# Layer 0's clamps of two sequences on GpSimd, and half of a folding sum in pieces between earlier matmuls, in a bidirectional minGRU and ternary feed-forward kernel

## The chip, the cores and the metric

The kernel runs on one core of a Trainium2 chip. The core has five engines with instruction lists of their own: TensorE (PE in the profile; its weight loads are PEld), VectorE (DVE), ScalarE (ACT), GpSimd (POOL) and SyncE (SP, which here only issues transfers). Engines wait for each other by semaphores. The metric is the device time of one execution in microseconds (us), lower being better; times given are medians of several runs.

## The reference

The input `x` is 8 sequences of 512 positions with 512 features, all in float32. Two stages are added to it.

```python
def _mingru(x, Wz, bz, Wh, bh):
    z = sigmoid(x @ Wz.T + bz)
    h_tilde = tanh(x @ Wh.T + bh)
    a = clip(1.0 - z, 1e-8, 1.0 - 1e-8)
    return linear_scan(a, z * h_tilde)        # h[s] = a[s] * h[s-1] + b[s]

def _stack(x):                                # four layers
    h = x
    for i in range(4):
        h_new = _mingru(h, W[i], b[i], W[i], b[i])
        if i > 0:
            h_new = h_new + h
        h = layernorm(h_new, gamma, beta)
    return h

n = layernorm(x)
h = concat(_stack(n), flip(_stack(flip(n))))  # forwards and backwards
x = x + h @ fusion_W.T + fusion_b
f = gelu(layernorm(x) @ ternary(W_fc).T)
x = x + (layernorm(f) * ln_w + ln_b) @ ternary(W_proj).T
```

Both gates of a layer use the same weights and bias, so one product `u` serves both, and forwards and backwards use the same weights too: in layer 0 they differ only in the direction of the scan. `ternary` rounds weights to -1, 0 and 1 by the mean of their absolute values.

## The kernel before

**Tiles.** A state is a tile of 128 partitions with 4 chunks of 512: the features lie along partitions (chunk `c` holds features 128c to 128c + 127), the 512 positions along the free dimension. A chunk of a layer is four matmuls of 128x128 by 128x512 in float32, added up in one PSUM tile `u` (L459 in layers 1 to 3, L504 in layer 0). The pool of these tiles, `ps_u`, has four buffers (L229). ScalarE makes the three factors from `u` (L476 to L478): `a`, the sigmoid of the negated sum, then `t`, the tanh, and `z`, the sigmoid. VectorE clamps `a` to the reference's limits (L482), multiplies `z` by `t` (L483) and scans (L487).

**Layer 0** (`first_layer`, L491) does not normalise `x` itself. Its weights are centred beforehand (L716), and VectorE multiplies `u` by the row of reciprocal deviations, `scale`, on its way out of PSUM (L515); the factors are then made from that SBUF tile. One set of factors serves a forward scan into `zf` and a backward scan into `z`. The three steps of a chunk stand in different slots: the matmuls in one, `scaled` later (by two slots for sequence 1), and `scans` one after that.

**The layer norm between layers** turns tiles of features into tiles of tokens: TensorE transposes four 128x128 blocks into a PSUM tile `pt` (L314), VectorE takes mean and variance (`stats`, L169 to L180), GpSimd raises the variance to the power -0.5 (L176, one number a partition), ScalarE writes the normalised `tok` (L186, L187), TensorE transposes back into `pf` (L323) and ScalarE applies gamma and beta (L329).

**Order.** The order of every engine's list is written out by hand by `slot` (L437): the matmuls of a chunk, then what is due by kind (`factors`, `late`, and so on), then shares of the transposes of other states, then scans, then the ends of the shares. Each engine works through its list in order. `first_layer(0)` and `first_layer(1, 2)` are run first (L728), then layers 1 to 3 of sequences 0 and 1, forwards and backwards in turn: the states are called (0, 0), (0, 1), (1, 0) and (1, 1).

**The folding.** gamma and beta of the last layer norm are folded into the fusion's weights. For each half `d` of these weights, `fold_sums` (L667) multiplies them by a tile `both` that repeats beta and gamma 64 times each (L730), four matmuls of 128x512 into one `u` buffer, and ScalarE copies the result to a `tok` tile. In the kernel before, the two halves are done behind layer 1 of states (0, 0) and (0, 1) (L763).

**Loads.** SP issues nearly all loads. A queue of eight semaphores is reused in turn, so each issue also waits for the landing of the load eight places before it. gamma and beta (2 KB each) stand behind sequence 1's rows and its transposed input (L147 to L151).

Of the kernel before, what the change touches and what calls it, by code (L numbers as in the profile page):

```python
# [16 lines left out]
P = 128  # L17
# [7 lines left out]
def kernel(  # L25
# [114 lines left out]
    for first, second in (  # L140
# [3 lines left out]
        for q, (load, at) in ((nc.scalar, first), (nc.sync, second)):  # L144
            load(q, at)
    nc.sync.dma_start(out=gb, in_=gru_b)
    for t in range(NT):  # L147
        load_x("n", 1, t)
    load_xT(1)
    nc.sync.dma_start(out=gam, in_=gamma)  # L150
    nc.sync.dma_start(out=bet, in_=beta)  # L151
    fw = fusp.tile([P, 2 * NC_, H], F32, name="fw")
    nc.sync.dma_start(out=fb, in_=fus_b.broadcast_to([P, H]))
    nc.sync.dma_start(out=fw, in_=fus_wT.rearrange("(c p) h -> p c h", p=P))
# [72 lines left out]
    with rec:  # L227
# [209 lines left out]
        def slot(work=None, cap=1, long=False):  # L437

            end = work() if work is not None else None
            due("factors")  # L440
            due("late")
            if long:
                due("scans")
            last = shares(cap) + x_shares()
            due("scans")
            if end is not None:
                end()
            due("resid")
            for f in last:
                if f is not None:  # L450
                    f()
            now[0] += 1
# [25 lines left out]
            nc.scalar.activation(z, u, AF.Sigmoid, bias=gb[:, l, o : o + 1])  # L478
            return a, t

        def product(a, z, t):
            nc.vector.tensor_scalar(a, a, CLAMP_HI, CLAMP_LO, ALU.min, ALU.max)  # L482
            nc.vector.tensor_tensor(z, z, t, ALU.mult)  # L483

        def scan(dst, a, z, backward):
# [5 lines left out]
        def first_layer(b, lag=0):  # L491
# [4 lines left out]
            def chunk(o):  # L496
                def work():
                    while zlive[0] + 2 > ZT:
                        slot(None, 2)
                    zlive[0] += 2  # L500
                    name = f"{b}_0_{o}"
                    u = ps_u.tile([P, S], F32, tag="u", name=f"u_{name}")
                    for c in range(NC_):
                        nc.tensor.matmul(  # L504
                            u, lhsT=gw[0][:, c, ts(o, P)], rhs=xT[b][:, c, :],
                            start=(c == 0), stop=(c == NC_ - 1),
                        )
                        if (b, o, c) in midway:
                            midway.pop((b, o, c))()

                    wait = 1 if (b, o) == (0, 0) else 0

                    def scaled():
                        z = zp.tile([P, S], F32, tag="z", name=f"z_{name}")
                        nc.vector.tensor_tensor(z, u, scale[b], ALU.mult)  # L515
                        a, t = factors(z, z, 0, o, name)

                        def scans():
                            product(a, z, t)
                            f = zp.tile([P, S], F32, tag="z", name=f"zf_{name}")  # L520
                            scan(f, a, z, False)
                            zf.append(f)
                            if o == NC_ - 1:
                                state[b, 0] = xT.pop(b)
                                norm((b, 0), zf, f"{b}0_0", 2 if b == 1 else 1, 2 if b < 2 else 1)

                            def backward():
                                scan(z, a, z, True)
                                zb.append(z)
                                if o == NC_ - 1:  # L530
                                    norm((b, 1), zb, f"{b}1_0", 2 if b == 1 else 1, 2 if b < 2 else 1)
                            if b == 0:
                                stages.append((now[0] + 1, "resid", backward))
                            else:
                                backward()
                        stages.append((now[0] + 1 - wait, "scans", scans))
                    stages.append((now[0] + lag + wait, "factors", scaled))
                return work
# [125 lines left out]

        folded = {}

        def fold_sums(d):  # L667

            ps = ps_u.tile([P, H], F32, tag="u", name=f"pfold_{d}")
            for c in range(NC_):  # L670
                nc.tensor.matmul(
                    ps, lhsT=both[:, c, :, :].rearrange("p i r -> p (i r)"), rhs=fw[:, d * NC_ + c, :],
                    start=(c == 0), stop=(c == NC_ - 1),
                )
            folded[d] = tokp.tile([P, H], F32, tag="tok", name=f"fold_{d}")
            held[0] += 1
            nc.scalar.copy(folded[d], ps)

        def fold(d):

# [44 lines left out]
        take(xturns)  # L725
        midway[0, 1, 0] = lambda: take(xbacks)()
        f0, f1 = first_layer(0), first_layer(1, 2)
        for i, work in enumerate(f0 + f1):  # L728
            slot(work, 4 if i == NC_ + 1 else 2, i > NC_ + 1)
        for i, v in enumerate((bet, gam)):  # L730
            nc.vector.tensor_copy(both[:, :, i, :], v.unsqueeze(2).broadcast_to([P, NC_, 64]))
        for b in range(0, B, 2):
            last_pair = b + 2 == B
            if b == 0:
# [9 lines left out]
            for l in range(1, L):  # L744
# [5 lines left out]
                for s in ((b, 0), (b, 1), (b + 1, 0), (b + 1, 1)):  # L750
# [9 lines left out]
                    if last_pair and s == (b, 0) and l == L - 1:  # L760
                        norm_y(0)
                    layer(s, l)
                    if b == 0 and l == 1 and s[0] == 0:  # L763
                        fold_sums(s[1])
                    if b == 0 and l == 2:
                        if s[0] == 0:
                            fold(s[1])
# [263 lines left out]
```

## Time and profile before

| | before |
|---|---|
| median of 3 runs | 1717.03 us (1716.73 to 1717.18) |
| profiled execution, whole | 1717.09 us |
| its span, first to last instruction | 1715.1 us |
| TensorE busy | 1703.4 us (99%) |
| VectorE busy | 1452.0 us (85%) |
| ScalarE busy | 1073.7 us (63%) |
| GpSimd busy | 214.0 us (12%) |

Four kinds of view are used. The page gives sums for the whole span. The chain of work that ended last gives, from the last instruction backwards, what each step waited for; its lines are start, length, engine and line. The timeline gives an engine's instructions in order of time: start, length, engine, line, operation, output and inputs, shapes, how many of them follow each other, and in brackets the idle time before and what ended it. A matmul in float32 is two records of half its work. Its end is modelled, so an idle time of TensorE is a little longer than the bracket says. The windows give busy times of all engines by stretch:

```profile
20.00:36.00 16.00, 16.00 (x53) 8.12 (x52) 14.46 (x29) 9.59 (x21) 2.48 (x5) 1.00 0.87 317
36.00:52.00 16.00, 13.43 (x60) 7.73 (x59) 15.16 (x35) 14.38 (x27) 4.17 (x6) 1.00 0.00 1
52.00:71.00 19.00, 18.82 (x56) 8.88 (x55) 18.59 (x26) 14.87 (x28) 0.00 (x0) 1.00 0.09 28
71.00:91.80 20.80, 19.36 (x75) 10.26 (x74) 19.39 (x48) 17.99 (x36) 4.82 (x8) 1.00 0.04 13
91.80:110.00 18.20, 18.20 (x81) 10.83 (x80) 13.70 (x35) 15.63 (x30) 3.62 (x6) 1.00 0.10 31
```

The columns are the stretch and its length, busy time and number of instructions of PE, PEld, DVE, ACT and POOL, the granted TensorE clock as a share, the mean share of the DMA engines and the rate in GB/s. In the first 92 us VectorE is busy over 90% of the time, and TensorE has pauses from 36 us on; behind that TensorE has none.

### The profile page before, as it was taken

Reading aid. Unit: us, or ns where it says so; the run is one execution under the profiler, and the core shown is the slowest. Engines: PE = TensorE matmul, PEld = TensorE weight load, DVE = VectorE, ACT = ScalarE, POOL = GpSimd, SP = SyncE. Lnnn points to the kernel's source line nnn. Section 1 sums busy time; section 2 is a strip of 40 time slices with the busy share of each in tenths; the row PEclk is TensorE's granted clock in tenths of the full one; section 3 lists DMA queues with packets and bytes.
Section 4 is the critical chain, followed back from the end, with each engine's and each line's share of the span. In section 5 each row is a group of like instructions: output and inputs, shape, how many; then the busy total and the mean of one; then the engine's idle time right before and its main releaser. Section 6 shows DMA issues by size and latency. Waiting matters only on the chain.

```text
span 1715.1 us, 19769 instructions
## 1 busy us (share of the span) xinstructions
PE 1703.4 (99%) x6440; PEld 1042.3 (61%) x6440; DVE 1452.0 (85%) x2863; ACT 1073.7 (63%) x1856; POOL 214.0 (12%) x334
## 2 busy tenths in 40 slices
PE   9999999999999999999999999999999999999999
PEld 4455554555555445555545555554688888888887
DVE  7989989889998998999899899996568768768877
ACT  5898873468886246888624688860366566566654
POOL 2111111111111111111111111110000000000000
PEclk9999999999999999999999999999999999999999
DMA  7002221160000115000011201202201101100100
GB/s 270 19 25 81 99 86 43 56 202 1 1 13 19 56 56 202 1 1 18 14 55 68 105 9 41 74 1 96 76 1 49 50 0 50 49 16 35 50 19 32
DMA packets 46599, 91.75 MB, mean 53 GB/s; under 512 B 5280, under 2 KB 5536, under 8 KB 45472
## 3 DMA queue, kind: packets, MB, share of 16 engines
q1 hardware_dynamic: 45488, 88.78, 15.1%
q10 hardware_dynamic: 1008, 1.70, 0.3%
q8 instruction: 51, 0.84, 0.2%
q14 instruction: 52, 0.43, 0.1%
HBM read 65.30 MB, written 25.17 MB: 53 GB/s over the span
## 4 chain that ended last, share of the span: by engine, by line
PE 87%; DVE 10%; ACT 1%; issue 1%; DMA 1%; POOL 0%; DVEq 0%; ACTq 0%
PE u L459 32%; PE po L870 14%; PE ph L843 14%; PE pu L586 12%; PE pt L314 6%; PE u L504 5%; PE pf L323 4%; DVE z L487 3%; DVE st L169 1%; DVE z L483 1%; PE py L212 1%; DVE zf L487 1%; DVE z L552 1%; DVE a L482 1%; DVE mv L171 0%
## 5 line engine op out<-in xcount | busy, mean ns | idle before, releaser
L459 PE MATMUL u<-h,gw 128*128 128x512 f32 x768 | 345.5, 592 | 0.0
L459 PE MATMUL u<-xT,gw 128*128 128x512 f32 x768 | 345.4, 593 | 0.0
L487 DVE TENSOR_TENSOR_SCAN z<-a,z 128x512 f32<-128x512 f32 x224 | 274.1, 1224 | 7.6
L459 PEld LDWEIGHTS u<-h,gw 128*128 128x128 f32 x768 | 138.7, 190 | 139.2 <-issue 138.9
L459 PEld LDWEIGHTS u<-xT,gw 128*128 128x128 f32 x768 | 138.7, 190 | 139.2 <-issue 138.2
L476 ACT ACTIVATE a<-u,ngb 128x512 f32<-128x512 f32 x192 | 131.6, 685 | 142.4 <-PE u L459 141.8
L169 DVE BATCH_NORM_STATS2 st<-pt 128x6 f32<-128x512 f32 x256 | 177.2, 692 | 40.8 <-PE pt L314 40.3
L176 POOL TENSOR_TENSOR rs<-ve,mhalf 128x1 f32<-128x1 f32 x192 | 122.7, 639 | 703.7 <-DVE nmu L180 665.4
L870 PE MATMUL po<-pwq,ghi 128*128 128x512 f32 x512 | 202.7, 396 | 0.0
L843 PE MATMUL ph<-yhi,fcq 128*128 128x512 f32 x512 | 199.7, 390 | 0.0
L870 PE MATMUL po<-pwq,glo 128*128 128x512 f32 x512 | 199.6, 390 | 0.0
L843 PE MATMUL ph<-ylo,fcq 128*128 128x512 f32 x512 | 199.4, 389 | 0.0
L847 ACT ACTIVATE g<-ph 128x512 f32<-128x512 f32 x128 | 76.4, 597 | 186.4 <-PE ph L843 186.4
L483 DVE TENSOR_TENSOR z<-z,t 128x512 f32<-128x512 f32 x224 | 153.4, 685 | 9.4 <-ACT z L478 9.4
L187 ACT ACTIVATE tok<-pt,nmr,rs 128x512 f32<-128x512 f32 x192 | 149.2, 777 | 6.4
L858 DVE TENSOR_TENSOR acc<-acc,g 128x512 f32<-128x512 f32 x112 | 77.3, 690 | 84.7 <-ACT g L847 83.8
L478 ACT ACTIVATE z<-u,gb 128x512 f32<-128x512 f32 x192 | 132.2, 689 | 0.0
L477 ACT ACTIVATE t<-u,gb 128x512 f32<-128x512 f32 x192 | 130.7, 681 | 0.0
L314 PEld LDWEIGHTS pt<-ident,z 128*128 128x128 f32 x640 | 78.6, 141 | 80.2 <-issue 47.5
L504 PE MATMUL u<-xT,gw 128*128 128x512 f32 x256 | 115.0, 593 | 1.0 <-DVE gw L716 0.8
L586 PE MATMUL pu<-fw,xT 128*128 128x512 f32 x256 | 115.2, 593 | 0.0
L586 PE MATMUL pu<-fw,h 128*128 128x512 f32 x256 | 115.1, 592 | 0.0
(150 smaller groups left out, 2559.8 us busy)
## 6 DMA issues: line engine op xcount, KB each, us to landing
xf<-in_x_dram SPq DMA_DIRECT2D x32, 256.0 KB, 5.8
x<-xf SPq DMA_DIRECT2D x32, 256.0 KB, 2.0
xy<-x SPq DMA_DIRECT2D x32, 256.0 KB, 4.1
xn<-in_x_dram SPq DMA_DIRECT2D x31, 256.0 KB, 4.5
out_dram<-xy SPq DMA_DIRECT2D x31, 256.0 KB, 2.0
xT<-in_xt_dram SPq DMA_DIRECT2D x7, 1024.0 KB, 7.5
fca<-in_fc_wT_dram SPq DMA_DIRECT2D x16, 256.0 KB, 3.0
pwa<-in_proj_wT_dram SPq DMA_DIRECT2D x16, 256.0 KB, 2.7
```

The lines of the kernel that those rows point to most:

```text
L169: nc.vector.bn_stats(st, src)
L187: nc.scalar.activation(dst, src, AF.Identity, bias=nmr, scale=rs)
L314: nc.tensor.transpose(pt[:, ts(c, P)], zs[c][:, ts(t, P)], ident)
L459: nc.tensor.matmul(u, lhsT=gw[l][:, c, ts(o, P)], rhs=h[:, c, :], start=(c == 0), stop=(c == NC_ - 1),)
L476: nc.scalar.activation(a, u, AF.Sigmoid, bias=ngb[:, l, o : o + 1], scale=-1.0)
L478: nc.scalar.activation(z, u, AF.Sigmoid, bias=gb[:, l, o : o + 1])
L483: nc.vector.tensor_tensor(z, z, t, ALU.mult)
L487: nc.vector.tensor_tensor_scan(dst[:, d], a[:, d], z[:, d], 0.0, ALU.mult, ALU.add)
L504: nc.tensor.matmul(u, lhsT=gw[0][:, c, ts(o, P)], rhs=xT[b][:, c, :], start=(c == 0), stop=(c == NC_ - 1),)
L586: nc.tensor.matmul(pu, lhsT=hs[d][:, c, ts(t, P)], rhs=fw[:, d * NC_ + c, :], start=(c == 0), stop=(c == NC_ - 1),)
L843: nc.tensor.matmul(ph, lhsT=w, rhs=ys[b][c][i], start=(c == 0 and i == 0), stop=(c == NC_ - 1 and i == 1),)
L870: nc.tensor.matmul(po[b][t], lhsT=part[:, ts(t, P)], rhs=pwq[k // NP_][:, k % NP_, :], start=(k == 0 and i == 0), stop=(k == NF - 1 and i ...
```

## The change

Two things are moved. First, the clamps of layer 0 of sequences 0 and 1, eight of them, go from VectorE to GpSimd: `scaled` queues a new kind of due work, `clamps`, which `slot` calls behind `late`, and `product` leaves the clamp out for them. Second, the second half of the folding's sums, for `d` = 1, is cut: two of its four matmuls come behind chunk 2 of layer 0 of sequence 1, one behind chunk 3, and the last behind the first half, which stays behind layer 1 of (0, 0). The PSUM tile stays open in between. For this `both` is filled earlier, behind the first chunk's multiplication by `scale`, and gamma's and beta's loads go ahead of sequence 1's rows in SP's list. The number of instructions stays the same.

```diff
     nc.sync.dma_start(out=gb, in_=gru_b)
+    nc.sync.dma_start(out=gam, in_=gamma)
+    nc.sync.dma_start(out=bet, in_=beta)
     for t in range(NT):
         load_x("n", 1, t)
     load_xT(1)
-    nc.sync.dma_start(out=gam, in_=gamma)
-    nc.sync.dma_start(out=bet, in_=beta)
...
             due("factors")
             due("late")
+            due("clamps")
             if long:
                 due("scans")
...
-        def product(a, z, t):
-            nc.vector.tensor_scalar(a, a, CLAMP_HI, CLAMP_LO, ALU.min, ALU.max)
+        def clamp(engine, a):
+            engine.tensor_scalar(a, a, CLAMP_HI, CLAMP_LO, ALU.min, ALU.max)
+
+        def product(a, z, t, early=False):
+            if not early:
+                clamp(nc.vector, a)
             nc.vector.tensor_tensor(z, z, t, ALU.mult)
...
                         a, t = factors(z, z, 0, o, name)
 
+                        if b < 2:
+                            stages.append((now[0], "clamps", lambda: clamp(nc.gpsimd, a)))
+                        if wait:
+                            for i, v in enumerate((bet, gam)):
+                                nc.vector.tensor_copy(both[:, :, i, :], v.unsqueeze(2).broadcast_to([P, NC_, 64]))
+
                         def scans():
-                            product(a, z, t)
+                            product(a, z, t, b < 2)
...
-        def fold_sums(d):
-
-            ps = ps_u.tile([P, H], F32, tag="u", name=f"pfold_{d}")
-            for c in range(NC_):
+        fold_ps = {}
+
+        def fold_sums(d, cs=range(NC_)):
+
+            for c in cs:
+                if c == 0:
+                    fold_ps[d] = ps_u.tile([P, H], F32, tag="u", name=f"pfold_{d}")
                 nc.tensor.matmul(
-                    ps, lhsT=both[:, c, :, :].rearrange("p i r -> p (i r)"), rhs=fw[:, d * NC_ + c, :],
+                    fold_ps[d], lhsT=both[:, c, :, :].rearrange("p i r -> p (i r)"), rhs=fw[:, d * NC_ + c, :],
                     start=(c == 0), stop=(c == NC_ - 1),
                 )
-            folded[d] = tokp.tile([P, H], F32, tag="tok", name=f"fold_{d}")
-            held[0] += 1
-            nc.scalar.copy(folded[d], ps)
+            if c == NC_ - 1:
+                folded[d] = tokp.tile([P, H], F32, tag="tok", name=f"fold_{d}")
+                held[0] += 1
+                nc.scalar.copy(folded[d], fold_ps[d])
...
         f0, f1 = first_layer(0), first_layer(1, 2)
+        def with_sums(work, d, cs):
+
+            def go():
+                end = work()
+                fold_sums(d, cs)
+                return end
+            return go
+
+        f1[2] = with_sums(f1[2], 1, (0, 1))
+        f1[3] = with_sums(f1[3], 1, (2,))
         for i, work in enumerate(f0 + f1):
             slot(work, 4 if i == NC_ + 1 else 2, i > NC_ + 1)
-        for i, v in enumerate((bet, gam)):
-            nc.vector.tensor_copy(both[:, :, i, :], v.unsqueeze(2).broadcast_to([P, NC_, 64]))
...
                     layer(s, l)
-                    if b == 0 and l == 1 and s[0] == 0:
-                        fold_sums(s[1])
+                    if b == 0 and l == 1 and s == (0, 0):
+                        fold_sums(0)
+                        fold_sums(1, (3,))
```

## Prediction

> **What bounds the kernel now.** First the page's busy times and its chain of work.
>
> ```profile
> PE 1703.4 (99%) x6440; PEld 1042.3 (61%) x6440; DVE 1452.0 (85%) x2863; ACT 1073.7 (63%) x1856; POOL 214.0 (12%) x334
> PE 87%; DVE 10%; ACT 1%; issue 1%; DMA 1%; POOL 0%; DVEq 0%; ACTq 0%
> ```
>
> TensorE sets the end nearly everywhere; only what shortens the stretch in which it waits can be gained. The chain, in order of time, says where that is:
>
> ```profile
> 21.43 0.15 DVE ve_x L383
> 21.58 0.33 DVE a L482
> ...
> 78.54 0.67 POOL rs L176
> ...
> 86.05 0.66 PE pt L314 x4
> ...
> 87.58 3.44 PE pfold L671 x8
> ```
>
> From 21.4 to 78.5 us it runs through VectorE, the clamps among it; from 86 us on through TensorE, the second half of the sums first. The timeline of PE shows the price of that stretch:
>
> ```profile
> 38.25 0.76 PE L314 MATMUL pt<-ident,z 128*128 128x128 f32 x5 [1.73 <-DVE z L487]
> ...
> 50.93 3.60 PE L459 MATMUL u<-xT,gw 128*128 128x512 f32 x8
> ...
> 75.18 0.66 PE L314 MATMUL pt<-ident,zf 128*128 128x128 f32 x4 [0.59 <-ACT tok L187]
> ...
> 80.39 0.66 PE L314 MATMUL pt<-ident,z 128*128 128x128 f32 x4 [0.59 <-ACT tok L187]
> ```
>
> With the smaller ones (0.39, 0.10, 0.34, 0.17, 0.26) TensorE stands 4.2 us here, and afterwards hardly (1.7 us in the next 1,600). VectorE's timeline has the other half: no idle time over 0.3 us between 21.4 and 91.8, and then
>
> ```profile
> 94.92 0.70 DVE L169 BATCH_NORM_STATS2 st<-pt 128x6 f32<-128x512 f32 x1 [3.13 <-PE pt L314]
> ```
>
> That is the length of the sums at 87.42 (3.43 us). So VectorE is the bound up to 91.8 and then gets a rest because TensorE does the sums. With them gone, a VectorE at the same point lets TensorE go on 3.43 us sooner. Call d how late VectorE stands, against before, at its first statistic of the next tokens (before: 70.88), from where it is busy without a break to 91.8. Then the gain is 3.43 - d, less a little.
>
> [...] The trace agrees for GpSimd as the loser, in POOL's timeline:
>
> ```profile
> 37.08 1.45 POOL L176 TENSOR_TENSOR rs<-ve,mhalf 128x1 f32<-128x1 f32 x1 [0.59 <-DVE nmu L180]
> 39.93 0.55 POOL L176 TENSOR_TENSOR rs<-ve,mhalf 128x1 f32<-128x1 f32 x1 [1.40 <-DVE nmu L180]
> ```
>
> The first power began 0.10 us into a scan (36.98 to 38.20) and ended 0.33 after it. At 1555.38 another began under one accumulation (to 1555.88), and ended at 1556.29 although a second one followed at once[...]. That second one kept its 0.69 us, but a power reads one element a lane and a clamp 512[...].
>
> [...] No clamp of GpSimd is in the trace. [...] The power's fixed part here is about 0.40 us (0.55 for 1 column; 1.02 for 4 at L889, so 0.155 each). I take a hold R [...] of 0.6 us, [...] and 1.0 us a clamp.
>
> **The change part by part.** All shifts are against the profiled execution, 1717.09 us, its span 1715.1 and 2.0 around it; the median of the runs is 1717.03, so the same sums hold for it.
>
> *Loads.* gamma's and beta's loads move two places ahead in SP's queue, before sequence 1's rows, whose first load is issued at 8.1 and lands 4.1 later, at 12.2. VectorE takes it at 12.68 behind other work. The queue moves about 390 GB/s there and a 2 KB load adds about 0.25, so the row lands near 12.7: nothing to 0.3 us, and the latter falls into VectorE's idle times at 16.87 (1.27) and 20.30 (0.55). Taken as 0; xT of sequence 1 and the weights land over 5 us before use.
>
> *The two copies of `both`* (0.40 at 47.29) move to 15.6, into the idle 1.27: -0.40.
>
> *Clamps.* Eight leave VectorE. A clamp costs it 0.33 us (21.50 to 21.83, start to start). The first (17.48) stood in a wait for ScalarE and brings nothing. On GpSimd each meets VectorE so:
> - sequence 0, chunk 0 and 1: beside idle time. Hold 0.
> - chunk 2: its `a` is ready at 22.0, behind a power that waits for the product; [...] Cost R. Chunk 3 the same before that of 27.64. Cost R.
> - So at the last scan of sequence 0 (36.98) VectorE stands s = 2R - 3 x 0.33 = +0.2.
> - sequence 1, chunks 0 and 1: ready at 40.28 and 45.58, under statistics and L515[...]. Hold 0. The powers behind them in POOL's list (39.93, 41.08, 46.25) start later, by up to 1.5 us. ScalarE calls for the first two at 42.88 and 43.88: covered, by 0.4 to 1 us.
> - chunk 2: ready at 52.6, in a product; the scan of 52.78 waits R. Chunk 3: ready near 58, in a scan; the next VectorE work waits R.
>
> ScalarE is fully busy from 38.57, where it waits for the power held by that scan, to 62.7, so it moves with s. VectorE meets it at 52.06 (product of layer 1, chunk 0, behind ScalarE's `z`, 51.31 to 52.01): what VectorE had saved meanwhile is lost in that wait, and it stands at s again. Then two holds and two clamps less: d = s + 2R - 0.66 = 4R - 1.65 = 0.75.
>
> *The sums.* Four products of 0.86 us leave 87.42. Two go behind chunk 2 and fill the wait at 36.5 (1.72 in 1.73). One goes behind chunk 3; it delays the transpose of 44.0 to about 45, which costs VectorE 0.4 us of idle at its statistic of 45.02, absorbed by the meeting at 52.06. The last stands behind the first half at 66.
>
> Their result stays in one of the four `u` buffers from 36 to 67 us, and this makes a new wait: layer 1's chunk 1 takes the buffer of chunk 0. It waits in the changed program for ScalarE's last read of it, before for VectorE's L515 at 47.7. That read ends at 52.01 + s = 52.2; TensorE was there at 50.93 and would now be at about 51.3. So it stands 0.9. From 52.2: two chunks, 16 and 8 transposes, first half, last piece, next chunk (3.43 each, 0.86 a piece or 8 transposes) puts the transposes for the statistic of 70.88 at 71.8 instead of 70.1. Their wait gives d = s + 0.72 = 0.92, larger than 0.75. So d = 0.92: TensorE, not the clamps, decides it narrowly.
>
> *Sum.* 3.43 - 0.92 = 2.5; VectorE's later start against TensorE after 91 costs about 0.1. Gain 2.4 us (0.14%): 1717.03 - 2.4 = 1714.6.
>
> In general d = max(4R - 1.65, 2R - 0.28)[...].
>
> **Rivals.** 0.2% of this kernel (3.43 us) is about what a measurement can tell from no change.
>
> 1. *VectorE isn't held up.* Its operations keep their times beside a long GpSimd read, as they did beside the power. Then s is about -0.65 (the transposes of 30.84 allow no more) and d about 0.07: 3.3 us, and if ScalarE is early too, so that the new wait for the buffer shrinks, up to 4.2: 1713.4. For it: the 0.69 us at 1555.79. Against it: [...] VectorE's 20.9 us without a gap after 70.88, where the change takes nothing.
>
> 2. *GpSimd's clamp is about 1.1 us of hold*, or the whole instruction counts: d = 2.35 to 3, gain 0.3 to 1: 1716.4. [...]
>
> 3. *Slower: GpSimd becomes the bound.* Four holds lie on VectorE's path, so above R = 1.3 the clamps cost more than the moved sums bring, and from (3.43 + 1.65 + 3.43) / 4 = 2.1 us on the time is over 0.2% slower. With 2.6 us [...]: d = 8.8, 5.4 us slower: 1722.4. [...]
>
> 4. *The change doesn't help*, the rows of sequence 1 land over 1 us late and the whole of VectorE's stretch starts late. Against it: the queue is kept full, and over 1 us of idle follows. This is kept in 2's time.
>
> **How the numbers follow.** Forecast (R of 0.4 to 0.9): 0.47, own range 1714.2 to 1715.7. Rival 1: 0.30, all of it close to the bound of 0.2%. Rivals 2 and 4: 0.13. Rival 3: 0.10, of which 0.01 stays within the bound. The shifts are read to about 0.3 us each and several add up, so the sum is good to some 1 us: beyond the bound lie two in three of rival 1 (0.20) and one in four of the forecast (0.12). Faster by over 0.2%: 0.32. Slower: 0.09. Within: 0.59. The range takes in a gain of 4.2 with no hold at all, and R up to about 1.3, and so 1712.8 to 1717.3, leaving out rival 3 and the far end of rival 1.
>
> **What would show it.** The wait of 1.73 at 38.25 gone to 0.3 or less; a new one of about 1 us before a matmul of L460 near 51.3, ended by ScalarE's `z`; a VectorE scan near 23.7, 27.6 and 53 that starts, or lasts, R longer; VectorE's wait before 94.9 gone; clamps on POOL of about 1 us. Wrong, if no scan is late (rival 1), if POOL's clamps last over 1.5 us (2, 3), or if the matmul near 51 doesn't wait, so that d comes from elsewhere.

## The result, and the profile after

The changed kernel takes 1715.01 us (median of 22 runs, 1714.68 to 1715.45) beside 1717.01 for the kernel before (22 runs, 1716.73 to 1717.92): 2.0 us less, ratio 0.9988 with a 95% interval of 0.9982 to 0.9993. That is faster, by less than the 0.2% that I had set as the bound of "no change". The forecast was 1714.6. The profiled execution, the slowest of the 22, took 1715.45 us with a span of 1712.9; the span of before was 1715.1.

The page of the changed kernel, busy times and chain:

```profile
PE 1702.7 (99%) x6440; PEld 1042.6 (61%) x6440; DVE 1451.3 (85%) x2855; ACT 1073.9 (63%) x1856; POOL 221.7 (13%) x342
...
PE 86%; DVE 9%; ACT 2%; issue 1%; DMA 1%; POOL 0%; DVEq 0%; ACTq 0%
```

TensorE is the bound as before; DVE's part of the chain went from 10% to 9%. The timeline of PE shows what became of the waits (the bracket at the end is TensorE's idle time before the row, and what ended it):

```profile
51.66 3.70 PE L460 MATMUL u<-xT,gw 128*128 128x512 f32 x8 [0.97 <-ACT z L479]
...
80.54 0.66 PE L314 MATMUL pt<-ident,z 128*128 128x128 f32 x4 [0.53 <-ACT tok L187]
...
86.21 0.66 PE L314 MATMUL pt<-ident,z 128*128 128x128 f32 x4 [0.27 <-ACT tok L187]
...
189.09 0.33 PE L323 MATMUL pf<-ident,tok 128*128 128x128 f32 x1 [0.24 <-ACT tok L187]
```

The 1.73 us before 38.25 is gone, and so is the 0.59 before the transposes of 75.18. A new wait of 0.97 us stands at 51.66, where one of 0.9 was forecast. A second new one stands at 189.09, where nothing was. VectorE's rest behind the moved sums, 3.13 us before 94.92, is gone too; in the changed kernel the same statistic follows at once on the work before it (90.95 and 0.69):

```profile
90.95 0.69 DVE L563 TENSOR_TENSOR z<-z,h 128x512 f32<-128x512 f32 x1
91.65 0.70 DVE L169 BATCH_NORM_STATS2 st<-pt 128x6 f32<-128x512 f32 x1
```

The new instructions are the clamps on GpSimd. From POOL's timeline, four of the eight:

```profile
16.76 0.61 POOL L483 TENSOR_SCALAR a<-a 128x512 f32<-128x512 f32 x1 [0.81 <-ACT a L477]
...
22.99 1.24 POOL L483 TENSOR_SCALAR a<-a 128x512 f32<-128x512 f32 x1
27.04 1.24 POOL L483 TENSOR_SCALAR a<-a 128x512 f32<-128x512 f32 x1
...
52.38 1.62 POOL L483 TENSOR_SCALAR a<-a 128x512 f32<-128x512 f32 x1 [4.72 <-ACT a L477]
```

Undisturbed, a clamp of 512 elements takes 0.61 us. Those that begin inside a scan of VectorE last until 0.40 to 0.42 us after its end (the scan at 22.60, for instance, ends at 23.83, the clamp at 24.23). VectorE's timeline has the other side, the scans and the two operations that come next to such a clamp:

```profile
23.74 1.56 DVE L492 TENSOR_TENSOR_SCAN z<-a,z 128x512 f32<-128x512 f32 x1
...
27.79 1.57 DVE L492 TENSOR_TENSOR_SCAN z<-a,z 128x512 f32<-128x512 f32 x1
...
53.63 0.92 DVE L563 TENSOR_TENSOR z<-z,xT 128x512 f32<-128x512 f32 x1
...
58.24 0.77 DVE L483 TENSOR_SCALAR a<-a 128x512 f32<-128x512 f32 x1
```

The same two scans in the kernel before, at 23.69 and 27.64:

```profile
23.69 1.20 DVE L487 TENSOR_TENSOR_SCAN z<-a,z 128x512 f32<-128x512 f32 x1
...
27.64 1.20 DVE L487 TENSOR_TENSOR_SCAN z<-a,z 128x512 f32<-128x512 f32 x1
```

So GpSimd, coming first, does hold VectorE up, by 0.36 us (1.56 - 1.20), which is close to the 0.33 that a clamp costs on VectorE. One more hold fell where the prediction had none, on the forward scan of sequence 0's chunk 0, which took 1.23 us in the kernel before (at 18.53):

```profile
18.73 0.61 POOL L483 TENSOR_SCALAR a<-a 128x512 f32<-128x512 f32 x1 [1.36 <-ACT a L477]
...
18.86 1.55 DVE L492 TENSOR_TENSOR_SCAN zf<-a,z 128x512 f32<-128x512 f32 x1
```

It costs nothing, because VectorE is idle for 0.68 us shortly after. It lasts 0.32 us, although 0.48 of the clamp was still to run when the scan began.

**One table for all runs.** The gain can be followed through five points: VectorE's `ve_x` (21.43 in the kernel before), the scan of `z_0_3` (36.98), the first statistic of the next tokens (70.88), TensorE's matmul `u` (90.85) and the end of the span. Each figure is worked out from two traces, as the start of the instruction in that kernel less its start in the kernel before, and then the difference from one point to the next; negative is sooner. "Around" is the mean of time less span over a kernel's runs (2.05 for the kernel before in one group, 2.04 and 2.03 in the others). "Time" is the difference of the medians of one group.

| kernel | to 21.4 | 21.4 to 37 | 37 to 71 | 71 to 91 | from 91 on | span | around | time |
|---|---|---|---|---|---|---|---|---|
| changed | +0.31 | -0.72 | +0.83 | -3.70 | +1.10 | -2.18 | 2.47 | -2.00 |
| changed, again | -0.29 | -0.73 | +0.82 | -3.71 | +1.02 | -2.89 | 2.43 | -2.00 |
| sums alone | -0.15 | +0.05 | +0.84 | -3.41 | +0.56 | -2.11 | 2.03 | -2.19 |
| clamps alone | +0.15 | -0.72 | +0.09 | -0.27 | +0.92 | +0.17 | 2.47 | +0.05 |
| four clamps | -0.25 | -0.92 | +0.85 | -3.71 | +0.61 | -3.42 | 2.18 | -3.27 |
| own columns (on before) | +0.17 | -0.65 | -0.03 | -0.28 | -1.57 | -2.36 | 2.04 | -2.76 |
| 16 clearings | +0.17 | -0.73 | +0.83 | -3.71 | +0.34 | -3.10 | 2.23 | -2.82 |
| closed early | +0.17 | -0.72 | +0.74 | -3.71 | +1.04 | -2.48 | 2.39 | -2.14 |
| closed in its slot | -0.10 | -0.73 | +0.74 | -3.73 | +1.06 | -2.76 | 2.40 | -2.19 |
| sums, own columns | -0.14 | -0.65 | +0.82 | -3.70 | -1.29 | -4.96 | 2.01 | -4.74 |
| changed, own columns | +0.07 | -0.72 | +0.83 | -3.70 | -1.27 | -4.79 | 2.27 | -4.53 |
| four clamps, own columns | -0.20 | -0.92 | +0.83 | -3.71 | -1.24 | -5.24 | 1.98 | -5.06 |

The first column is one execution's: the second execution of the changed kernel has it 0.6 us sooner than the first. The next three columns agree to 0.02 us wherever the instructions of that stretch are alike, so they can be read closely.

### The profile page after: what moved, and what is told of

Its sections match the earlier page's. It is cut to its first block, busy times and chain, and to the rows that moved or that the text cites. A ratio compares the mean times of both kernels' runs of the same rounds, so it can differ in the third digit from the quotient of the medians.

```text
span 1712.9 us, 19759 instructions
## 1 busy us (share of the span) xinstructions
PE 1702.7 (99%) x6440; PEld 1042.6 (61%) x6440; DVE 1451.3 (85%) x2855; ACT 1073.9 (63%) x1856; POOL 221.7 (13%) x342
## 4 chain that ended last, share of the span: by engine, by line
PE 86%; DVE 9%; ACT 2%; issue 1%; DMA 1%; POOL 0%; DVEq 0%; ACTq 0%
PE u L460 32%; PE po L894 14%; PE ph L867 14%; PE pu L597 12%; PE pt L314 5%; PE u L509 4%; PE pf L323 4%; DVE z L492 2%; DVE st L169 2%; DVE z L488 1%; PE py L212 1%; ACT tok L187 1%; DVE z L563 1%; DVE a L483 1%; DVE zf L492 1%
## 5 line engine op out<-in xcount | busy, mean ns | idle before, releaser
L460 PE MATMUL u<-xT,gw 128*128 128x512 f32 x768 | 345.5, 593 | 1.0 <-ACT z L479 1.0
L460 PE MATMUL u<-h,gw 128*128 128x512 f32 x768 | 345.5, 592 | 0.0
L460 PEld LDWEIGHTS u<-xT,gw 128*128 128x128 f32 x768 | 138.6, 190 | 139.9 <-issue 138.0
L460 PEld LDWEIGHTS u<-h,gw 128*128 128x128 f32 x768 | 138.7, 190 | 139.2 <-issue 138.9
```

What stands on the lines that cost most here:

```text
L460: nc.tensor.matmul(u, lhsT=gw[l][:, c, ts(o, P)], rhs=h[:, c, :], start=(c == 0), stop=(c == NC_ - 1),)
```

## The experiments

### Which part brings the gain: sums alone, clamps alone

The first takes the changed kernel and gives VectorE its clamps back; the second takes the kernel before and moves only the eight clamps.

```diff
-                        if b < 2:
-                            stages.append((now[0], "clamps", lambda: clamp(nc.gpsimd, a)))
...
-                            product(a, z, t, b < 2)
+                            product(a, z, t)
```

```diff
+            due("clamps")
...
+        def clamp(engine, a):
+            engine.tensor_scalar(a, a, CLAMP_HI, CLAMP_LO, ALU.min, ALU.max)
...
+                        if b < 2:
+                            stages.append((now[0], "clamps", lambda: clamp(nc.gpsimd, a)))
...
-                            product(a, z, t)
+                            product(a, z, t, b < 2)
```

> The changed kernel with all clamps back on VectorE: loads, copies and sums in pieces stay. Theory A (a GpSimd clamp holds VectorE up by 0.34 us, no more than the 0.33 us it saves, so the clamps are nearly a wash, and most of the gain is the sums'): VectorE keeps the second wait of its small `ve` operations, so the scan of z_0_3 ends near 37.0 + 0.2 (loads) less the clamp... about where it was before; the new wait for the `u` buffer stays, about 1.0 us at 51.7, d is 0.7 to 1.0, the span's gain is 1.4 to 2.0 us: ratio 0.9988 to 0.9992. Theory B (the clamps on GpSimd are what brings VectorE forward): the gain falls to under 0.8 us, ratio above 0.9995. Theory C (the clamps still cost VectorE more than they save): the gain is larger than the changed kernel's 2.2 us, ratio under 0.9985.

> The kernel before with only the eight clamps of the first two sequences on GpSimd: loads, copies of gamma and beta and sums as before. No piece of the sums holds a `u` buffer, so no wait of over 0.3 us before the matmul near 51. Theory A (wash, but for the lost second waits of `ve`): VectorE's first statistic of the next tokens (70.88 before) comes 0.3 to 0.9 us sooner, and the span ends 0.3 to 0.9 sooner: ratio 0.9995 to 0.9998. Theory B (clamps are what brings VectorE forward): over 1.0 us, ratio under 0.9994. Theory C (clamps cost VectorE more than they save): no gain or a loss, ratio 1.0000 or above.

Sums alone: 1714.88 us (21 runs), ratio 0.9986 (0.9980 to 0.9993). Clamps alone: 1717.12 us (13 runs) beside 1717.07, ratio 0.9999 (0.9991 to 1.0008). So the sums bring what the change brings, and the clamps nothing. Theory A came nearest for the sums (a gain of 1.4 to 2.0 us in the span, where the profile has 2.11), but had expected up to 0.9 us of the clamps. The table shows that they do bring it and lose it again: from the start of `ve_x` to 91 us the clamps alone gain 0.90 us (0.72 - 0.09 + 0.27); from 91 on 0.92 is lost, and 0.42 more lies around the span. (The profiled execution of the clamps alone, 1717.75 us, was the slowest of its 13, so these figures add up to more than the difference of the medians.) The place of the loss is TensorE's timeline at 191 us, in clamps alone:

```profile
191.28 0.33 PE L323 MATMUL pf<-ident,tok 128*128 128x128 f32 x1 [0.28 <-ACT tok L187]
```

130 us after the last of these clamps a wait appears that the kernel before doesn't have. In sums alone there is none. The buffer wait, in turn, is there with sums alone, and not with the clamps:

```profile
51.98 3.70 PE L460 MATMUL u<-xT,gw 128*128 128x512 f32 x8 [0.97 <-ACT z L479]
```

### What a hold costs: only the clamps of chunks 0 and 1 on GpSimd

```diff
-                        if b < 2:
+                        quiet = b < 2 and o < 2
+                        if quiet:
...
-                            product(a, z, t, b < 2)
+                            product(a, z, t, quiet)
```

> The changed kernel with only the clamps of chunks 0 and 1 of the two sequences on GpSimd (those that I had put down as holding nothing up); chunks 2 and 3 are clamped by VectorE. Theory A (hold 0.34 us is equal to the clamp's 0.33): the four scans of 23.7, 27.8, 53.6 and the clamp of 58.2 have their short times again (1.22, 1.22, 0.69, 0.40), VectorE has four clamps of 0.33 us more, and the time is the changed kernel's within 0.3 us: ratio 0.9986 to 0.9990. Theory C (the hold costs more than the clamp, R of 0.6): 0.5 to 1.0 us faster than the changed kernel, ratio 0.9982 to 0.9985. Theory B (GpSimd's clamps are a gain each): 0.5 to 1.3 us slower than it, ratio 0.9991 to 0.9996.

1713.80 us (13 runs), ratio 0.9980 (0.9972 to 0.9988). The two scans that were held up, in VectorE's timeline of this kernel:

```profile
23.18 1.20 DVE L492 TENSOR_TENSOR_SCAN z<-a,z 128x512 f32<-128x512 f32 x1
...
27.13 1.20 DVE L492 TENSOR_TENSOR_SCAN z<-a,z 128x512 f32<-128x512 f32 x1
```

Their holds are gone. By the table the stretch up to 37 us is 0.20 us shorter than with all eight clamps, although VectorE has two clamps of 0.33 more in it: two clamps on GpSimd cost 0.86 us there (0.66 + 0.20), 0.43 each. Measured from start to start, a held backward scan accounts for 0.37 of it (the next operation starts 1.49 us after it, instead of 1.12). Nearly all of the rest is a wait in front of the forward scan: this scan now waits for GpSimd's clamp, and the trace has an instruction ahead of it that only waits (the scan starts 0.77 us after the product before it, instead of 0.72). In the stretch of sequence 1 (37 to 71) two clamps more or less make no difference (0.85 against 0.83): VectorE isn't the bound there. But the time is 1.3 us less than the changed kernel's in its own group, which no theory had; theory C's 0.5 to 1.0 came nearest, and for a reason that isn't its own: 0.4 to 0.5 us of the saving lies after 91 us (0.61 lost instead of 1.0 to 1.1), and 0.25 to 0.29 around the span. Some 0.3 to 0.4 us of it lies in none of these stretches and stays unplaced.

### Where the unforeseen 0.65 us come from: `ve` without a second wait

The scan of `z_0_3` came sooner than the clamps allow. In the kernel before, VectorE's `ve` (the variance plus epsilon) goes into one of eight rotating buffers, so it waits for GpSimd's power to have read an older one, besides waiting for `mv`. The trace has an instruction of its own for it that only waits, ahead of each such `ve` (16 of 16 between 21 and 91 us). Where VectorE's scans already wait for GpSimd's clamps, that of `ve` is left out (in the changed kernel none of these 16 has one). The experiment takes it away without touching the clamps:

```diff
+    ves, n_ve = const.tile([P, 140], F32, name="ves"), [0]
...
-        ve = small.tile([P, 1], F32, tag="ve", name=f"ve_{name}")
+        n_ve[0] += 1
+        if n_ve[0] > 140:
+            ve = small.tile([P, 1], F32, tag="ve", name=f"ve_{name}")
+        else:
+            ve = ves[:, n_ve[0] - 1 : n_ve[0]]
```

> The kernel before, but the first 140 `ve` results are columns of one tile, so none of them waits for GpSimd to have read an earlier one. Theory V (a second wait costs VectorE's `ve` operation about 0.07 us each time, and its loss explains the 0.4 us by which the scan of z_0_3 came sooner than the holds allow): the gap between `mv` and `ve` falls from 0.11 to 0.03 us in the first 90 us, VectorE's first statistic of the next tokens comes 0.8 to 1.5 us sooner than 70.88, and the span ends 0.5 to 1.2 us sooner: ratio 0.9993 to 0.9997. Rival (the gap is not the wait's; it shrank in the changed kernel for another reason, such as GpSimd's own timing): gap stays 0.11, ratio 1.0000 within 0.0002.

1714.31 us (18 runs), ratio 0.9983 (0.9976 to 0.9990): 2.8 us, more than twice what was expected, out of an edit that leaves every operation as it is. The groups of instructions between 21 and 91 us, the row of `ve` (busy time, mean ns, idle time just before it), of the kernel before:

```profile
L175 DVE TENSOR_SCALAR ve<-mv 128x1 f32<-128x1 f32 x16 | 2.5, 154 | 1.7
```

and of this one:

```profile
L181 DVE TENSOR_SCALAR ves<-mv 128x1 f32<-128x1 f32 x16 | 2.5, 153 | 0.6
```

(1.7 - 0.6) / 16 = 0.07 us for each. In the changed kernel the row reads 0.6 as well. Four of them lie between 21 and 37 us (0.28). Of the eight between 71 and 91 TensorE sees four: by its own timeline it stands 0.65 us sooner than before at 75.18, 0.79 at 80.39 and still 0.79 at 90.85, 0.28 more than VectorE's 0.51 at 70.88 (the fifth column; 0.27 for the clamps alone). The rest of the 0.65 is one late start of VectorE, which the kernel before has and this one doesn't:

```profile
34.26 0.14 DVE L180 TENSOR_SCALAR nmu<-mv 128x1 f32<-128x1 f32 x1
34.68 0.70 DVE L169 BATCH_NORM_STATS2 st<-pt 128x6 f32<-128x512 f32 x1 [0.28 <-issue]
```

By its usual distance from `nmu` (it starts 0.06 us after the start of `nmu`, at 33.18 for instance) this statistic is 0.36 us late, and waits for nothing. 0.28 + 0.36 = 0.64. From 91 us on the columns bring 1.57 more, where I had looked for little: VectorE is busy for 90% of that stretch up to 600 us (in the changed kernel 101 us of the 109 from 91 to 200, 360 of the next 400), so that it runs close behind TensorE, and what a `ve` saves can count. Not all of the 1.57 is the second waits': the late starts of the next section that the kernel before has at 96.31, 210.63, 334.88 and 397.99 us are gone as well. How much each brings wasn't separated.

### Why 1 us is given back after 91: late starts in VectorE's list

Such late starts have places. I counted VectorE's records in the traces, the ones that only wait included (3,403 in the kernel before, 3,387 in the changed one): those late by 0.28 us or more, with nothing to wait for, right behind a `mv`, `ve` or `nmu`, are the 64th, 192nd, 320th, and so on in steps of 128: all 78 of them after 25 us, over thirteen traces (7 in the kernel before, 8 in the changed one, 3 where `ve` has columns of its own). Each has the waiting instruction of a `ve` one to three records ahead of it. At the other such places, where a scan or a product stands before or the `ve` nearby has no waiting instruction of its own, nothing is late without a wait. (One other kind of instruction can be late there, if it has a waiting instruction of its own: `xf` at place 2496 of the changed kernel, 1219.96 us, by 0.35.) Eight clamps less, and eight waits less on balance, move everything behind them by 16 places. Six of the places:

| place | kernel before: start, instruction, late | changed kernel |
|---|---|---|
| 64 | 34.68 `st`, 0.36 | 34.42 `st`, 0 |
| 192 | 96.31 `ve`, 0.36 | 98.29 `nmu`, 0.34 |
| 320 | 152.32 scan, 0 | 158.02 `ve`, 0.35 |
| 448 | 210.63 `nmu`, 0.32 | 212.81 `st_x`, 0.29 |
| 960 | 458.62 scan, 0 | 463.89 clamp, 0.29 |
| 1088 | 517.04 `st`, 0 | 520.81 `ve`, 0.37 |

In the changed kernel's timeline of VectorE, place 320:

```profile
157.38 0.18 DVE L171 BATCH_NORM_AGGREGATE mv<-st 128x2 f32<-128x6 f32 x1
158.02 0.15 DVE L175 TENSOR_SCALAR ve<-mv 128x1 f32<-128x1 f32 x1 [0.46 <-DVE mv L171]
```

The profile puts the idle time down to `mv`, which had ended 0.46 us before. TensorE's wait at 189.09 follows: VectorE has no idle time in which to make the 0.35 us good. The experiment puts 16 one-column clearings into VectorE's list before its first statistics, which moves the places back and changes nothing else:

```diff
     nc.vector.memset(mhalf, -0.5)
+    pad = const.tile([P, 16], F32, name="pad")
+    for i in range(16):
+        nc.vector.memset(pad[:, i : i + 1], 0.0)
```

> The changed kernel with 16 clearings of one column each put into VectorE's list before its first statistics, where it has nothing to do. Theory P (VectorE starts its 64th, 192nd, 320th instruction and so on in steps of 128, waits counted, up to 0.37 us late if short instructions stand before it; the clamps' leaving moved these places by 16, and the losses of 0.40 us at 189 and 0.33 at 523 follow from it): the places lie again where they lay in the kernel before, so the late `ve` near 158.0 and 520.8 are gone, no wait of TensorE near 189 and 523, and the time is 0.5 to 0.8 us under the changed kernel's: near 1714.4. Rival (those losses come from the clamps themselves, or by chance): the two waits stay and the time is the changed kernel's within 0.2 us.

1714.01 us (18 runs) beside 1714.83 for the changed kernel on the same chip: 0.82 us faster with 16 instructions more (1713.82 to 1714.40 against 1714.51 to 1715.21). The same `ve` in this kernel's timeline starts 0.11 us after `mv` ends, as most do:

```profile
157.21 0.18 DVE L174 BATCH_NORM_AGGREGATE mv<-st 128x2 f32<-128x6 f32 x1
157.50 0.15 DVE L178 TENSOR_SCALAR ve<-mv 128x1 f32<-128x1 f32 x1
```

TensorE's wait near 189 is gone, and from 91 on 0.34 us is lost instead of 1.0 to 1.1; another 0.2 of the 0.82 lies around the span. Theory P holds: the loss goes with the place in the list.

What happens at every 128th record can be read in part from the traces, which also list DMA packets by kind. The page of the kernel before has this among its queues (number of packets, MB, share):

```profile
q14 instruction: 52, 0.43, 0.1%
```

In the trace these are 52 packets of 8,192 bytes, one for every 128 records in the lists of VectorE, ScalarE, GpSimd and SyncE together (6,758 / 128 = 52.8). Behind 77 of the 78 late starts such a packet begins 0.6 to 1.1 us later, and behind one 2.0 us later; for the `st` at 34.68 it is the one at 35.34. So my estimate is that the late start is VectorE's call for its next 128 instructions, and that a longer instruction just ahead hides it. That rests on these times going together: no run took the call away.

### The loads: the changed kernel again

> The changed kernel once more, beside the others of this group. It is to separate what its first profile owed to that one execution (rows of sequence 1 landed 5.3 us after their issue there, 3.7 to 3.8 in two kernels with the same loads) from what it owes to its instructions. Theory L (the loads' new place makes the rows late): landing again over 5 us, VectorE's `ve_x` of 21.43 again at 21.7. Theory N (that landing was one execution's): landing near 3.8, `ve_x` at 21.2 to 21.5. The time is 1715.0 again either way; the stalls of VectorE before the `ve` at 158.0 and at 520.8 (0.35 us each) are there again.

1714.83 us (21 runs) beside 1716.83. SyncE's seven loads of rows, three of sequence 0 and four of sequence 1, landed 4.0 us after their issue (median; 5.3 in the first execution), the last of them at 15.43 us (17.15 in the first). `ve_x`, which follows on ScalarE's work on the rows, in the second execution and then in the first:

```profile
21.14 0.15 DVE L383 TENSOR_SCALAR ve_x<-ss_x 128x1 f32<-128x1 f32 x1 [0.43 <-ACT xn L380]
```

```profile
21.74 0.15 DVE L383 TENSOR_SCALAR ve_x<-ss_x 128x1 f32<-128x1 f32 x1 [0.68 <-ACT xn L380]
```

Theory N: the same program, 0.6 us apart. Over the nine kernels that have the early loads, `ve_x` starts 0.29 us sooner to 0.31 later than before; the new place of the two loads costs nothing that can be seen.

### Is it the `u` buffer? The sums closed earlier

In the next two kernels pieces 2 and 3 both stand behind chunk 3, so that nothing of these sums is left for 66 us. In the first, ScalarE's copy comes one slot later, as in this diff; the second has `now[0]` in place of `now[0] + 1`, which puts it into the same slot.

```diff
-        f1[3] = with_sums(f1[3], 1, (2,))
+        f1[3] = with_sums(f1[3], 1, (2, 3))
...
-                        fold_sums(1, (3,))
...
-                nc.scalar.copy(folded[d], fold_ps[d])
+                copy = lambda: nc.scalar.copy(folded[d], fold_ps[d])
+                if d:
+                    stages.append((now[0] + 1, "resid", copy))
+                else:
+                    copy()
```

> The changed kernel with the fourth piece of the sums behind chunk 3 beside the third, so that their buffer is free some 20 us sooner; ScalarE's copy of the result is put one slot later. Theory T (TensorE's wait of 0.97 us before the matmul of L460 sets how late VectorE stands after 70 us): that wait falls below 0.3 us, VectorE's first statistic of the next tokens comes 0.3 to 0.6 us sooner, the time is 0.2 to 0.6 us under the changed kernel's. Theory V (VectorE is late by its own work there): the wait goes, VectorE's statistic stays where it is, and the time stays within 0.2 us. Theory S (ScalarE's list is full there and a copy of 0.57 us more in it is what shows): 0.2 to 0.6 us slower than the changed kernel.

> As the kernel with the fourth piece beside the third, but ScalarE's copy of the sums in the same slot, so that the `u` buffer is read out near 47 us, before layer 1's chunk 1 asks for one at 51. Theory T (the buffer is what TensorE waits for at 51, and this wait is the 0.83 us by which VectorE falls back between 37 and 71 us in every kernel with the sums in pieces): no wait over 0.3 us before the matmul of L460 near 51, and VectorE falls back 0.2 to 0.6 us there; time 0.2 to 0.6 us under the changed kernel's 1714.9. Theory S (ScalarE's list is what sets TensorE's pace there): the wait goes, but another of 0.4 us or more comes before a matmul near 47 to 48, VectorE falls back 0.8 us or more as before, and the time is the changed kernel's within 0.2 us or above.

Closed early: 1714.69 us (21 runs); the copy ran at 54.04, too late, and TensorE still waited:

```profile
52.21 3.70 PE L460 MATMUL u<-xT,gw 128*128 128x512 f32 x8 [1.06 <-ACT z L479]
```

That run says nothing on the buffer. Closed in its slot: 1714.68 us (21 runs), and the wait is gone; the first idle time of TensorE over 0.2 us after 20 us is now

```profile
54.57 1.33 PE L323 MATMUL pf<-ident,tok 128*128 128x128 f32 x8 [0.26 <-ACT h L329]
...
74.95 0.66 PE L314 MATMUL pt<-ident,zf 128*128 128x128 f32 x4 [0.56 <-ACT tok L187]
```

Yet VectorE falls back by 0.74 us between 37 and 71, against 0.83: a gain of 0.09 for a wait of 0.97. In the changed kernel its first statistic of the next tokens waits for TensorE:

```profile
71.30 0.70 DVE L169 BATCH_NORM_STATS2 st<-pt 128x6 f32<-128x512 f32 x1 [0.69 <-PE pt L314]
```

Closed in its slot, the same statistic starts at 70.79 and waits for nothing: VectorE itself is late. It falls back at another point. Against the kernel before, its product of 52.06 (behind ScalarE's `z`) goes from 0.83 us sooner at 37 to 0.15 sooner in this kernel, and from 0.55 sooner to 0.13 later in the one before; in the changed kernel it doesn't move (0.41 and 0.42 sooner). What the two have in common is the fourth piece behind chunk 3, 0.86 us of TensorE ahead of layer 1's chunk 0. Counted from `ve_x`, the matmuls of that chunk start 0.82 us later than in the changed kernel (25.07 against 24.25), and the product 0.68 later. So neither theory holds in full: the buffer is what TensorE waits for at 51, and giving it back doesn't pay, most likely because the piece that was behind 66 costs about as much where it was put. A third place for it wasn't tried.

### What the clamps are worth without their side effects

Three kernels with the columns of their own for the first 140 `ve`, so that no late start and no second wait comes or goes with the clamps in the first 400 us: all clamps on VectorE, all eight on GpSimd, four on GpSimd. Each is the edit of `ve` above on the kernel of that name.

> Sums in pieces and early loads as in the changed kernel, all clamps on VectorE, and the first 140 `ve` results in columns of their own. Theory A (what the clamps on GpSimd brought up to 37 us, 0.72 us, is nearly all the loss of the second wait of four `ve` and of one late start of VectorE; columns of their own bring the same): scan of z_0_3 0.65 us nearer to the start of `ve_x` than before, gain near 2.2 + 0.9 (two stretches up to 91 us) or more, since later waits go too: ratio 0.9970 to 0.9980. Theory B (the clamps' leaving itself brought VectorE forward): no better than the sums alone, 0.9986.

> The changed kernel with the first 140 `ve` results in columns of their own, so that no second wait is left in the first 400 us with or without clamps. Set beside the kernel with the same columns and all clamps on VectorE it shows what the eight clamps on GpSimd are worth by themselves. Theory A (a hold costs what a clamp costs): the scan of z_0_3 within 0.15 us of that kernel's, against the start of `ve_x`, the time within 0.3 us. Theory B (the clamps bring 0.7 us by themselves): 0.6 to 0.8 us faster than it. Theory C (they cost): over 0.3 us slower.

> The same columns, and only the clamps of chunks 0 and 1 of the first two sequences on GpSimd, where VectorE was not held up or had time. Theory A: 0.2 to 0.35 us faster than with all clamps on VectorE (one clamp of 0.33 us that costs nothing), up to 37 us: 0.9 us nearer to the start of `ve_x` than before. Time by the sum of the two edits run before: ratio 0.9965 if they add up, 0.9970 to 0.9980 if TensorE is the bound by then. Theory B (each clamp on GpSimd is a saving): slower than the kernel with all eight by 0.3 us or more.

| clamps on GpSimd | time, us | ratio, interval | 21.4 to 37 |
|---|---|---|---|
| none | 1712.13 (7 runs) | 0.9973, 0.9962 to 0.9983 | -0.65 |
| eight | 1712.34 (8 runs) | 0.9973, 0.9963 to 0.9983 | -0.72 |
| chunks 0 and 1 | 1711.81 (6 runs) | 0.9971, 0.9959 to 0.9982 | -0.92 |

Theory A in all three: eight clamps on GpSimd bring VectorE 0.07 us up to 37 us and cost 0.2 us of time (by the last but one column of the first table, around the span); the four that cost VectorE no time bring 0.27 and 0.32. The 0.07 adds up from start to start: three clamps less on VectorE (0.98), two holds (0.74), and the waiting instructions ahead of three forward scans (0.17). The 0.2 us of time are less sure, since the runs with none and with eight overlap (1711.97 to 1712.40 and 1712.22 to 1712.52). With none of them, the sums and the columns give 4.74 us, near the sum of the two edits run singly (2.19 + 2.76 = 4.95). The fastest kernel of this study is the last, 1711.81 us, 5.06 less than before. Its page and PE's timeline:

```profile
PE 1701.1 (99%) x6440; PEld 1042.6 (61%) x6440; DVE 1453.1 (85%) x2859; ACT 1072.9 (63%) x1856; POOL 214.9 (13%) x338
...
PE 94%; DVE 3%; ACT 1%; DMA 1%; issue 0%; POOL 0%; DVEq 0%; ACTq 0%; POOLq 0%
```

```profile
50.94 3.70 PE L466 MATMUL u<-xT,gw 128*128 128x512 f32 x8 [0.97 <-ACT z L485]
...
79.82 0.66 PE L320 MATMUL pt<-ident,z 128*128 128x128 f32 x4 [0.52 <-ACT tok L193]
85.49 0.66 PE L320 MATMUL pt<-ident,z 128*128 128x128 f32 x4 [0.27 <-ACT tok L193]
```

VectorE has gone from 10% of the chain to 3%, and these are the only idle times of TensorE over 0.2 us between 20 us and the end.

## Why the prediction was right, and where it was not

The forecast (1714.6) and its range held, and the likeliest case, faster by less than 0.2%, came about. The sum got there by terms of which three were wrong and nearly cancelled, so that its coming out so close is luck:

| term of the gain, us | forecast | first profile of the changed kernel |
|---|---|---|
| sums leave 87.42 | 3.43 | 3.43 |
| start of that execution | 0 | -0.31 |
| VectorE, 21 to 37 (-s) | -0.20 | +0.72 |
| VectorE, 37 to 71 | -0.72 | -0.83 |
| VectorE, 71 to 91 | 0 | +0.27 |
| after 91 | -0.1 | -1.10 |
| span | 2.4 | 2.18 |

To this come 0.42 us around the span (2.47 against 2.05 on average), so that the medians differ by 2.0.

- *The bound, and the sums.* Right. VectorE's rest of 3.13 us and TensorE's 1.73 disappeared together, and sums alone give the whole gain.
- *The loads at nothing.* Right: the start varies by 0.6 us between executions of one program, about the same early point on average. The 0.25 us for a 2 KB load was my estimate; in the trace of before the packets of both loads take about that together (256 of 16 bytes, 240 of which begin between 16.30 and 16.55 us).
- *A hold of 0.6 us, a clamp of 1.0.* Neither was shown, nor were the 1.1 and 2.6 us of rivals 2 and 3: the trace of before has no clamp on GpSimd. VectorE does wait when GpSimd comes first (the scans of 23.74 and 27.79 last 1.56 and 1.57 us instead of 1.20), so rival 1 falls. The sizes were off: 0.61 us a clamp and 0.37 a hold, 0.43 with the wait in front of the forward scan. A hold is shorter than the clamp, and far from what rivals 2 and 3 need, so they fall too. The holds fell where they were put, before the backward scans of chunks 2 and 3, and for sequence 1 on `L563` and on a clamp of VectorE's own; one more fell on the forward scan of chunk 0 and cost nothing. The hold of 0 for sequence 1's chunks 0 and 1 is borne out: those clamps (40.04 and 45.34) took 0.61 and 0.62 us, and the statistics under which they began (39.67 and 44.85) 0.69 and 0.70, where the kernel before has 0.69 and 0.67.
- *s = 2R - 0.99 = +0.2.* This step failed. With R at 0.37 it is -0.25; measured from the start of the stretch it was -0.72. The waits in front of three forward scans take 0.17 back, so that the eight clamps themselves brought 0.07; four second waits of `ve` brought 0.28 and a late start at place 64 the other 0.36. None of these waits and late starts was in the sum.
- *TensorE, not the clamps, decides d: s + 0.72.* Right in size: 0.83 in every kernel with the sums in this place, whatever the clamps did in that stretch. The wait at `L460`, forecast at 0.9, was 0.97. That the buffer's wait is the price is only half the story: VectorE does wait for TensorE at 71.30, but with the buffer given back early VectorE was late by itself, and 0.74 of the 0.83 stayed.
- *"VectorE's later start against TensorE after 91 costs about 0.1."* This step failed: 1.0 to 1.1 us. About 0.3 of it comes at once, at the transposes that stand at 99.9 in the kernel before, and is there in sums alone too; 0.40 at 189 and 0.33 at 523 come with the late starts at places 320 and 1088, as the 16 clearings showed. That VectorE is close behind TensorE there could be seen before: the kernel before has waits of TensorE for this kind of work at 226.83 (0.28) and 373.85 (0.23).
- *Time is span plus 2.0.* Failed by 0.4 us. All kernels with the eight clamps have 2.2 to 2.5 us around the span, those with four 2.2 and 2.0, those with none 2.0. The traces show something that goes with it. The clamps lengthen GpSimd's list from 573 records to 578 or 580, past its place 576, which is again 64 and a multiple of 128. Where there are no clamps on GpSimd, no 8,192-byte packet of instructions begins behind the end of the span. In the kernels with 2.4 to 2.5 us around the span two begin there (in the changed kernel 0.97 and 2.24 us behind it), in the two with eight clamps and 2.2 to 2.3 us one. The two kernels with four clamps have two (2.2 us) and one (2.0 us). That these packets lengthen the time is likely, but no run was made for it.
- *Rival 4* falls with the loads.

What stays open: whether the call for instructions is what makes VectorE late at every 128th record and lengthens the time outside the span, as the times suggest; how the 1.57 us that the columns bring after 91 us divide between second waits and late starts; and why the sums' fourth piece costs as much in either of its two places.

## What to carry to other kernels

When an engine is the bound and runs many short instructions, count its waits as well as its operations: results in columns of their own instead of rotating buffers saved more here (2.8 us, late starts that went with them included) than moving work did (2.0). A piece of work moved to another engine brings its price less the hold (0.37 us for each of the two held scans here, beside a clamp's price of 0.33) and less the wait for it (0.06), so move only those pieces that meet idle time (0.32 us for four clamps, nothing for eight). And where a new wait appears far behind a change, compare the two lists instruction by instruction before looking for a cause in the work: here it was 16 places in a list.

## What the runs showed of the hardware that I had not expected

- In the kernel before, each `ve` between 21 and 91 us, which waits for GpSimd besides `mv`, has an instruction ahead of it that only waits: 0.07 us each, in 16 cases of 16 (0.106 or 0.107 us from the end of `mv` to `ve`, instead of 0.034 or 0.035 in the changed kernel, where none has one).
- In VectorE's list, the 64th record and every 128th after it starts 0.29 to 0.42 us late if the waiting instruction of a `ve` stands one to three records ahead of it, and on time behind a scan or a product (78 late starts in thirteen traces). An 8,192-byte packet of the instruction queue begins 0.6 to 1.1 us later in 77 of the 78. Shifting the list by 16 moved the late starts and gave 0.82 us.
- In the changed kernel GpSimd's clamp of 128x512 takes 0.61 us by itself, and 1.24 to 1.62 when it begins in the first half of a scan. VectorE's next scan lasts 0.36 us longer (1.56 instead of 1.20), less than the clamp's own length.
- The time around the span, 2.0 us without clamps on GpSimd, was 2.2 to 2.5 us with eight of them, and went with packets of the instruction queue that begin behind the end of the span.
